# Local attention's values: one product over a mixed block of keys, and two products in halves of TensorE's rows

## The chip, the cores and the metric

The kernel runs on one core of one Trainium2 chip, as one program. The metric is device time in microseconds (us), measured around one execution. Times in the tables come from the runs and from one profiled execution of the kernel before.

## What is computed

A decoder layer over `x` of 4 batches x 512 rows x 512, in three parts, each added to `x`: local attention with 16 heads of 128 that share one key and one value head, cross attention over 1024 context rows, and a ternary feed-forward network. The change touches the first part alone, cut here to what matters:

```python
k = _rmsnorm(_apply_partial_rope(h @ wk, cos, sin), k_norm_w)   # one key head for all 16 heads
v = h @ wv
diff = i[:, None] - i[None, :]
mask = (diff >= 0) & (diff < WIN)                                # WIN = 128
scores = jnp.einsum('bhtd,bsd->bhts', q, k) * scale
scores = jnp.where(mask[None, None], scores, -1e30)
probs = jax.nn.softmax(jnp.concatenate([scores, sink], axis=-1), axis=-1)
attn = jnp.einsum('bhts,bsd->bhtd', probs[..., :t], v)
```

Every row sees the 128 keys that end with itself. In tiles of 128 rows, row t of a tile sees keys 0 to t of its own tile and keys t+1 to 127 of the tile before it: for each place p among 128 exactly one of the two tiles' keys. So one 128x128 block holds all weights of a head's row tile, and the first row tile of a batch has no tile before it.

## The kernel before

The 2048 rows are 16 row tiles of 128, four to a batch. Local attention works in 64 `Unit`s: row tile `t` = n // 4 and head group `g` = n % 4, four heads (`HG`) each; `qt` is the tile's number in its batch. A unit goes through these steps:

- `queries`: `q_ps` (L770), rope on ScalarE and VectorE (L554 to L561), and the reciprocal root of the norm `rs` on GpSimd (L81).
- `turn`: four transposes of q (`qtr`, L780) and a copy `qT` on ScalarE (L782).
- `scores`: `sc` (L789) against the keys of both tiles; `s` takes the own tile's scores (L794) and, where the mask `older` says so, those of the tile before (L795, `neg_sb` in a batch's first tile); then the negative maxima `nm` (L799 to L801).
- `weights`: `p` by exponentials on ScalarE (L811), their sums `den` on VectorE, and the division on GpSimd (L818).
- `turn_weights`: four transposes of p into PSUM (`ptr`, L825); VectorE writes two masked copies, `pT[:, 1]` for keys of the own tile (`newer_t`, L827) and `pT[:, 0]` for keys of the tile before (`older_t`, L829, where `qt > 0`).
- `values`: `av` as the sum of a product with `v[:, qt]` (L834) and, where `qt > 0`, one with `v[:, qt - 1]` (L836); ScalarE copies it into `attnT` (L843).

When four units have filled a tile's `attnT`, `project` makes its output: 16 products `y` (L663), added to `xres` (L667). TensorE's and ScalarE's orders are written out by hand in one loop over n: unit n's `turn`, unit n-1's `weights`, unit n+1's `queries`, unit n's `scores`, unit n-2's `values`, unit n-1's `turn_weights`. `fill` puts pieces of work that is due at any time between them: first the folding of the output weights (L652), later the products `y`. Around `values` the loop reads:

```python
                if n >= 2:
                    units[n - 2].values()
                fill(1 if many else 1 + n % 2)
```

`before(b)` prepares the next batch's `qcT`, keys and `v` in the same loop (L587, `kv_ps` L601, `ktr` L619), `ternary_weights` reads and rounds the feed-forward weights on VectorE (L687 to L717), `mask_rows` has one small product of four rows (L757), and `first_rows` begins cross attention in the last steps (L189, L223, L290). VectorE's and GpSimd's orders are left to the scheduler.

PSUM has eight banks: pool `aq` holds one bank for `q_ps` and `qtr` (tag "q") and one for `ptr` and `av` (tag "p"); `asc` two for `sc`; `af` two for tag "f", which serves the preparation, and two for tag "y". Cross attention, from about 700 us, uses parts of TensorE's array: `weights` there runs four products on 32 rows each (L1051), and `weigh` and `divide` four products with 32 columns each (L1076, L1090).

Of the kernel before, what the change touches and what calls it, by code (L numbers as in the profile page):

```python
# [12 lines left out]
F32 = mybir.dt.float32  # L13
F32R = mybir.dt.float32r
BF16 = mybir.dt.bfloat16
U32 = mybir.dt.uint32
U8 = mybir.dt.uint8
AF = mybir.ActivationFunctionType
ALU = mybir.AluOpType
# [3 lines left out]
P = 128  # L23
# [5 lines left out]
HG = 4  # L29
# [21 lines left out]
def decoder_layer(  # L51
# [7 lines left out]
    nc = tc.nc  # L59
# [66 lines left out]
    def transpose_rows(pool, src, dst, tag="tr", copy=None):  # L126

        ps = pool.tile([P, DC, P], F32, tag=tag, name="tr_ps")
        for c in range(DC):
            nc.tensor.transpose(ps[:, c, :], src[:, ts(c, P)], ident)  # L130
        (copy or nc.scalar.copy)(dst, ps)
# [60 lines left out]
    class KeysValues:  # L192
# [62 lines left out]
        def values(self, quarter):  # L255
            if quarter == 0:
                self.va = values_pool["bp"].tile([P, KT, P], F32, name="va", bufs=2)
            v_ps = some_bank([P, 2, P], "v_ps")
            for i in range(2):
                for c in range(DC):  # L260
                    nc.tensor.matmul(
                        v_ps[:, i, :], lhsT=self.cxT[quarter][:, c, ts(i, P)], rhs=wv_sb[:, c, :],
                        start=(c == 0), stop=(c == DC - 1),
                    )
            nc.scalar.copy(self.va[:, 2 * quarter:2 * quarter + 2, :], v_ps)
# [220 lines left out]
    with tc.tile_pool(name="aw", bufs=1) as aw, tc.tile_pool(name="akv", bufs=2) as akv, \  # L486
# [15 lines left out]
        sin_sb = aw.tile([P, QT, 64], F32, name="sin_sb")  # L502
        nc.sync.dma_start(out=sin_sb, in_=c_sin.rearrange("(t p) n -> p t n", p=P))

        kq_col = aw.tile([P, 2], F32, name="kq_col")
        nc.sync.dma_start(out=kq_col[:, 0:1], in_=k_norm_w.rearrange("(p o) -> p o", o=1))
        nc.sync.dma_start(out=kq_col[:, 1:2], in_=q_norm_w.rearrange("(p o) -> p o", o=1))
        kw_col = aw.tile([P, 1], F32, name="kw_col")
# [9 lines left out]

        older = aw.tile([P, P], F32, name="older")
        nc.gpsimd.memset(older, 0.0)
        nc.gpsimd.affine_select(
            out=older, in_=older, compare_op=ALU.is_ge, fill=1.0, base=0,
            pattern=[[-1, P]], channel_multiplier=1,
        )
        older_t = aw.tile([P, P], F32, name="older_t")
        nc.gpsimd.memset(older_t, 1.0)
        nc.gpsimd.affine_select(
            out=older_t, in_=older_t, compare_op=ALU.is_gt, fill=0.0, base=0,  # L530
            pattern=[[-1, P]], channel_multiplier=1,
        )
        newer_t = aw.tile([P, P], F32, name="newer_t")
        nc.gpsimd.memset(newer_t, 0.0)
        nc.gpsimd.affine_select(
            out=newer_t, in_=newer_t, compare_op=ALU.is_gt, fill=1.0, base=0,
            pattern=[[-1, P]], channel_multiplier=1,
        )
        neg_sb = aw.tile([P, P], F32, name="neg_sb")
        nc.gpsimd.memset(neg_sb, NEG)  # L540

        def heads(ap):
            return ap.unsqueeze(1).to_broadcast([P, HG, P])
# [86 lines left out]
        def fold():  # L630
            w2s = {}

            def turned(n):
                g, h = divmod(n, HG)
                if h == 0:
                    w2s[g] = ap.tile([P, DC, D], F32, name="w2")
                    nc.sync.dma_start(
                        out=w2s[g], in_=out_w2[g * D:(g + 1) * D].rearrange("(c p) o -> p c o", p=P)
                    )
                w1 = ap.tile([P, D], F32, name="w1")  # L640
                nc.sync.dma_start(out=w1, in_=out_w1[g, ts(h, P)])
                w1T = ap.tile([P, DC, P], F32, name="w1T")
                transpose_rows(fp, w1, w1T, tag="y", copy=nc.vector.tensor_copy)
                return w1T

            w1T = turned(0)
            yield
            for n in range(HEADS):
                after = turned(n + 1) if n + 1 < HEADS else None
                f_ps = fp.tile([P, D], F32, tag="y", name="f_ps")  # L650
                for c in range(DC):
                    nc.tensor.matmul(  # L652
                        f_ps, lhsT=w1T[:, c, :], rhs=w2s[n // HG][:, c, :],
                        start=(c == 0), stop=(c == DC - 1),
                    )
                    yield
                nc.scalar.copy(wf[:, n, :], f_ps)
                w1T = after

        def project(t, attnT):  # L660
            y = fp.tile([P, D], F32, tag="y", name="y")
            for h in range(HEADS):
                nc.tensor.matmul(  # L663
                    y, lhsT=attnT[:, h, :], rhs=wf[:, h, :], start=(h == 0), stop=(h == HEADS - 1)
                )
                yield
            nc.vector.tensor_tensor(xres[:, t, :], y, xres[:, t, :], ALU.add)  # L667
# [95 lines left out]
        class Unit:  # L763
# [20 lines left out]
            def scores(self):  # L784
                g, qt, kT = self.g, self.qt, made[self.b][1]
                sc = scp.tile([P, HG, 2 * P], F32, name="sc")
                first = 1 if qt == 0 else 0
                for h in range(HG):
                    nc.tensor.matmul(  # L789
                        sc[:, h, first * P:], lhsT=self.qT[:, h, :],  # L790
                        rhs=kT[:, (qt - 1 + first) * P:(qt + 1) * P], start=True, stop=True,
                    )
                s = a2.tile([P, HG, P], F32, name="s")
                nc.scalar.copy(s, sc[:, :, P:2 * P])  # L794
                nc.vector.copy_predicated(  # L795
                    s, heads(older.bitcast(U32)), heads(neg_sb) if qt == 0 else sc[:, :, 0:P]
                )
                nm = small.tile([P, HG], F32, tag="nm", name="nm")
                nc.vector.tensor_reduce(nm, s, AX.X, ALU.max, negate=True)  # L799
                nc.vector.tensor_tensor(nm, nm, self.rs, ALU.mult)  # L800
                nc.vector.tensor_tensor(nm, nm, nsink_sb[:, ts(g, HG)], ALU.min)  # L801
                es = small.tile([P, HG], F32, tag="es", name="es")
                nc.vector.tensor_tensor(es, nm, sink_sb[:, ts(g, HG)], ALU.add)
                self.s, self.nm, self.es = s, nm, es
# [17 lines left out]
            def turn_weights(self):  # L822
                ptr = qp.tile([P, HG, P], F32, tag="p", name="ptr")
                for h in range(HG):
                    nc.tensor.transpose(ptr[:, h, :], self.p[:, h, :], ident)  # L825
                self.pT = a2.tile([P, 2, HG, P], F32, name="pT", bufs=1)
                nc.vector.tensor_tensor(self.pT[:, 1], ptr, heads(newer_t), ALU.mult)  # L827
                if self.qt > 0:
                    nc.vector.tensor_tensor(self.pT[:, 0], ptr, heads(older_t), ALU.mult)  # L829

            def values(self):
                v, qt = made[self.b][2], self.qt
                av = qp.tile([P, HG, P], F32, tag="p", name="av")
                nc.tensor.matmul(av, lhsT=v[:, qt, :], rhs=self.pT[:, 1], start=True, stop=(qt == 0))  # L834
                if qt > 0:
                    nc.tensor.matmul(  # L836
                        av, lhsT=v[:, qt - 1, :], rhs=self.pT[:, 0], start=False, stop=True
                    )
                if self.g == 0:
                    while self.t - 3 in behind:  # L840
                        fill(1)
                    attnTs[self.t] = a2.tile([P, HEADS, P], F32, name="attnT", bufs=3)
                nc.scalar.copy(attnTs[self.t][:, ts(self.g, HG), :], av)  # L843
                if self.g == G - 1:
                    behind[self.t] = project(self.t, attnTs.pop(self.t))

        attnTs, behind = {}, {"fold": fold()}

        def fill(n):

            for _ in range(n):
                while behind:
                    first = next(iter(behind))
                    if next(behind[first], "end") != "end":
                        break
                    del behind[first]

        with tc.manual_schedule(engines={mybir.EngineType.PE, mybir.EngineType.Activation}):
# [24 lines left out]
            for b in range(1, B):  # L883
                nc.sync.dma_start(
                    out=xres[:, b * QT:(b + 1) * QT, :], in_=x[b].rearrange("(t p) d -> p t d", p=P)
# [73 lines left out]
    with tc.tile_pool(name="b1", bufs=1) as b1, \  # L959
# [208 lines left out]
        for b in range(1, B):  # L1168
            at = KT * HG * (b - 1)
# [114 lines left out]
    with tc.tile_pool(name="c1", bufs=1) as c1, \  # L1284
# [14 lines left out]
        def tile_at(t):  # L1299
            return tiles[t] if 0 <= t < NT else Nothing()  # L1300
# [7 lines left out]
        for s in range(NT + 5):  # L1308
            now, prev, old, older, oldest = (tile_at(s - d) for d in range(5))
# [90 lines left out]
```

## Time and profile before

| | |
|---|---|
| median of 3 runs | 1709.8 us (1709.46 to 1713.5) |
| profiled execution | 1710.19 us, of which the span from first to last instruction is 1708.3 us |
| granted TensorE clock | 0.989 of full speed over the span |
| TensorE busy | 1632.2 us (96%) |
| VectorE, ScalarE, GpSimd busy | 1173.7, 919.8 and 707.8 us |
| `av` products (L834, L836) | 128 and 96 records of 592 ns, first at 73.0, last at 668.2 us |
| copies of `av` (L843) | 64, median 585 ns |
| masked copies (L827, L829) | 64 of 692 ns and 48 of 681 ns (medians) |

PE is TensorE's products, PEld its weight loads, DVE VectorE, ACT ScalarE, POOL GpSimd, SP the engine that issues most transfers. L12 is line 12 of the kernel. A product of f32 operands appears as two records on PE, each with a load on PEld. Ends of matmul records are modelled, so successive records overlap in the profile; the distance between starts tells how long one holds the array. In a timeline row the columns are start, length, engine, line, operation, operands, form and how many records were merged.

### The profile page before, as it was taken

To read this page: it belongs to the slowest core of one execution; us is meant where nothing else is said; L and a number is where in the kernel's file an instruction comes from. 1 tells how busy PE (TensorE), PEld (TensorE's weight loads), DVE (VectorE), ACT (ScalarE), POOL (GpSimd) and SP (SyncE) were. 2 spreads that over 40 slices of the span, in tenths; PEclk is the share of its full clock that TensorE was granted. 3 is DMA by queue.
4 is the path that set the end of the run, shared out by engine and by line. 5 is a ranking of instruction groups with operands and counts; after the bars stand their busy time and mean duration, and the time that the engine had idled before them with its cause. 6 is when DMAs were issued, how large, how long until landed. Compare 5 with 4: busy or idle time off the path is not lost.

```text
span 1708.3 us, 22965 instructions
## 1 busy us (share of the span) xinstructions
PE 1632.2 (96%) x7872; PEld 938.4 (55%) x7904; DVE 1173.7 (69%) x2323; ACT 919.8 (54%) x1807; POOL 707.8 (41%) x458
## 2 busy tenths in 40 slices
PE   7899999999999999899999999999999998999997
PEld 4555555655655555555555555555544435666664
DVE  4556886888787863565656666666657657989997
ACT  1444454555455553134544454445565764888885
POOL 2212222222222221347878787878778930000000
PEclk9999999999999999889999999999999999999999
DMA  8422221322233200412112111221121110000000
GB/s 258 136 88 85 74 75 52 84 81 72 78 74 93 68 1 25 100 54 52 52 32 60 50 47 37 56 54 33 39 69 55 35 57 2 13 13 14 19 19 25
DMA packets 96549, 99.56 MB, mean 58 GB/s; under 512 B 50884, under 2 KB 57672, under 8 KB 96008
## 3 DMA queue, kind: packets, MB, share of 16 engines
q1 hardware_dynamic: 88608, 84.30, 17.3%
q10 hardware_dynamic: 6672, 12.65, 2.3%
q0 software_dynamic: 1152, 1.15, 0.3%
q8 instruction: 62, 1.02, 0.2%
q14 instruction: 55, 0.45, 0.1%
HBM read 61.76 MB, written 10.86 MB: 43 GB/s over the span
## 4 chain that ended last, share of the span: by engine, by line
PE 80%; DVE 7%; ACT 6%; issue 3%; SPq 1%; DMA 1%; POOL 1%; ACTq 0%; POOLq 0%; DVEq 0%
PE y L663 12%; PE s_ps L992 8%; PE st L1040 7%; PE o_ps L1076 6%; PE sc L789 5%; PE q_ps L290 3%; PE f_ps L652 3%; PE xo_ps L1135 3%; PE av L834 3%; PE st L1051 3%; PE q_ps L770 3%; PE av L836 2%; PE y_ps L422 2%; PE d_ps L470 2%; ACT p L1058 2%
## 5 line engine op out<-in xcount | busy, mean ns | idle before, releaser
L1065 POOL TENSOR_TENSOR sum<-sum,p 128x1024 f32<-128x1024 f32 x180 | 423.1, 2377 | 37.3 <-ACT p L1058 37.1
L996 DVE TENSOR_REDUCE nm<-s_ps 128x1 f32<-128x512 f32 x512 | 319.7, 682 | 165.9 <-PE s_ps L992 165.8
L1058 ACT ACTIVATE p<-st 128x1024 f32<-128x1024 f32 x256 | 249.1, 1020 | 86.0 <-PE st L1051 81.8
L663 PE MATMUL y<-wf,attnT 128*128 128x512 f32 x512 | 246.8, 592 | 0.0
L818 POOL TENSOR_TENSOR p<-p,den 128x512 f32<-128x512 f32 x64 | 67.2, 1050 | 407.6 <-DVE den L817 230.1
L992 PE MATMUL s_ps<-ks,qs 99*128 99x512 f32 x512 | 200.1, 460 | 23.3 <-DVE nm L996 13.3
L992 PEld LDWEIGHTS s_ps<-ks,qs 99*128 99x128 f32 x512 | 88.6, 192 | 175.9 <-DVE nm L996 59.9
L1040 PE MATMUL st<-qs,ks 101*128 101x512 f32 x512 | 165.6, 404 | 5.3 <-ACT p L1058 3.8
L1076 PE MATMUL o_ps<-p,va 128*32 128x512 f32 x1024 | 137.3, 605 | 0.7 <-ACT p L1058 0.7
L663 PEld LDWEIGHTS y<-wf,attnT 128*128 128x128 f32 x512 | 91.9, 190 | 73.7 <-issue 71.7
L811 ACT ACTIVATE p<-s,nm,rs 128x128 f32<-128x128 f32 x256 | 123.2, 484 | 8.4 <-DVE nm L801 8.4
L1065 POOL TENSOR_TENSOR sum<-p,p 128x1024 f32<-128x1024 f32 x30 | 70.6, 2374 | 110.8 <-ACT p L1058 97.2
L1040 PEld LDWEIGHTS st<-qs,ks 101*128 101x128 f32 x512 | 95.6, 191 | 36.8 <-ACT p L1058 21.5
L789 PE MATMUL sc<-kT,qT 128*128 128x256 f32 (+1 forms) x512 | 107.6, 353 | 0.0
L789 PEld LDWEIGHTS sc<-kT,qT 128*128 128x128 f32 x512 | 88.8, 190 | 27.2 <-issue 17.9
L81 POOL TENSOR_TENSOR rs<-ss,neghalf 128x4 f32<-128x4 f32 (+1 forms) x72 | 80.2, 1115 | 53.5 <-DVE ss L564 50.8
L782 ACT COPY qT<-qtr 128x512 f32<-128x512 f32 x64 | 37.5, 585 | 114.1 <-PE qtr L780 111.6
L843 ACT COPY attnT<-av 128x512 f32<-128x512 f32 x64 | 37.5, 585 | 101.7 <-PE av L836 84.4
L386 PEld LDWEIGHTS <-xqT 128*128 128x128 bf16 x512 | 50.4, 99 | 48.8 <-issue 3.1
L827 DVE TENSOR_TENSOR pT<-ptr,newer_t 128x512 f32<-128x512 f32 x64 | 44.0, 688 | 43.7 <-PE ptr L825 43.5
L294 ACT ACTIVATE qH<-q_ps 128x256 fp32r<-128x256 f32 x32 | 12.3, 384 | 106.0 <-PE q_ps L290 102.6
L422 PE MATMUL y_ps<-had,mT 128*128 128x128 f32 x512 | 68.7, 282 | 0.0
(195 smaller groups left out, 3030.5 us busy)
## 6 DMA issues: line engine op xcount, KB each, us to landing
cx<-in_ctx SPq DMA_DIRECT2D x32, 256.0 KB
qs<-qH SPq DMA_DIRECT2D x128, 64.0 KB
w<-in_L_attn_out_w SPq DMA_DIRECT2D x4, 1024.0 KB
w<-in_L_attn_out_w SPq DMA_DIRECT2D x16, 256.0 KB
raw<-in_L_ffn_w_gate SPq DMA_DIRECT2D x4, 1024.0 KB
raw<-in_L_ffn_w_up SPq DMA_DIRECT2D x4, 1024.0 KB
raw<-in_L_ffn_w_down SPq DMA_DIRECT2D x4, 1024.0 KB
raw<-in_L_ffn_w_gate ACTq DMA_DIRECT2D x8, 512.0 KB
```

What stands on the lines that cost most here:

```text
L81: nc.gpsimd.tensor_tensor(dst, src, neghalf[:, :src.shape[1]], ALU.pow)
L422: nc.tensor.matmul(y_ps[:, k, :], lhsT=self.mT[q][:, k, :], rhs=had, start=True, stop=True)
L663: nc.tensor.matmul(y, lhsT=attnT[:, h, :], rhs=wf[:, h, :], start=(h == 0), stop=(h == HEADS - 1))
L789: nc.tensor.matmul(sc[:, h, first * P:], lhsT=self.qT[:, h, :], rhs=kT[:, (qt - 1 + first) * P:(qt + 1) * P], start=True, stop=True,)
L811: nc.scalar.activation(self.p[:, h, :], s[:, h, :], AF.Exp, bias=nm[:, h:h + 1], scale=self.rs[:, h:h + 1], accum_out=den[:, h:h + 1],)
L818: nc.gpsimd.tensor_tensor(self.p, self.p, den.unsqueeze(2).to_broadcast([P, HG, P]), ALU.mult)
L992: nc.tensor.matmul(s_ps, lhsT=qss[hh][0:R_TOP, g, ts(qt, P)], rhs=kss[b % 2][0:R_TOP, g, ts(hf, T)], start=True, stop=True,)
L996: nc.vector.tensor_reduce(nms[m][:, qt, g, hf:hf + 1], s_ps, AX.X, ALU.max, negate=True)
L1040: nc.tensor.matmul(st[:, g % 2, :], lhsT=ks[0:R_TOP + 2, g, ts(kt, P)], rhs=qss[hh][0:R_TOP + 2, g, :], start=True, stop=False,)
L1058: nc.scalar.activation(p, st, AF.Exp)
L1065: by.tensor_tensor(sums[m][i], last[i] if kt == 1 else sums[m][i], ps[i], ALU.add)
L1076: nc.tensor.matmul(accs[m][at, :], lhsT=va[:, kt, at], rhs=ps[g // 2][:, g % 2, :], start=(kt == 0), stop=(kt == KT - 1),)
```

## The change

The transposed weights are used in another grouping. Split the 128 key places and the 128 rows of a tile in halves of 64. For rows 0 to 63, places 64 to 127 are all keys of the tile before; for rows 64 to 127, places 0 to 63 are all keys of the own tile. A new tile `mixed`, made once for each row tile with `qt > 0` by two copies on GpSimd, holds the own tile's values in places 0 to 63 and the previous tile's in 64 to 127. One masked copy (`either_t`) leaves in `pT[:, 1]` all weights that go with `mixed`; what remains are two 64x64 corners a head, written to `pT[:, 0]` by two subtractions.

`values` now makes two tiles `av` of 64 rows each for the four heads (256 columns), one in the bank of tag "p", the other in one of tag "f". Two products over all 128 places run against `mixed` (or `v[:, 0]` in a batch's first tile), and where `qt > 0` two more over 64 places each, on partitions 0 to 63 and 64 to 127. ScalarE copies the two tiles with two instructions. The mask `older_t` goes, and the constant `neg_sb` becomes one column of `kq_col`, read with a broadcast.

```diff
-        older_t = aw.tile([P, P], F32, name="older_t")
...
+        either_t = aw.tile([P, P], F32, name="either_t")
+        nc.vector.tensor_copy(either_t[0:64], newer_t[0:64])
+        nc.vector.tensor_scalar(either_t[64:P], newer_t[64:P], -1.0, 1.0, ALU.mult, ALU.add)
+        neg_sb = kq_col[:, 2:3]
...
-                nc.vector.tensor_tensor(self.pT[:, 1], ptr, heads(newer_t), ALU.mult)
+                nc.vector.tensor_tensor(
+                    self.pT[:, 1], ptr, heads(either_t if self.qt > 0 else newer_t), ALU.mult
+                )
                 if self.qt > 0:
-                    nc.vector.tensor_tensor(self.pT[:, 0], ptr, heads(older_t), ALU.mult)
+                    for at in (slice(0, 64), slice(64, P)):
+                        nc.vector.tensor_tensor(
+                            self.pT[at, 0, :, at], ptr[at, :, at], self.pT[at, 1, :, at],
+                            ALU.subtract,
+                        )
...
-                av = qp.tile([P, HG, P], F32, tag="p", name="av")
-                nc.tensor.matmul(av, lhsT=v[:, qt, :], rhs=self.pT[:, 1], start=True, stop=(qt == 0))
+                if self.g == 0 and qt > 0:
+                    mixed[0] = a2.tile([P, P], F32, name="mixed", bufs=1)
+                    nc.gpsimd.tensor_copy(mixed[0][0:64], v[0:64, qt])
+                    nc.gpsimd.tensor_copy(mixed[0][64:P], v[64:P, qt - 1])
+                avs = [
+                    pool.tile([P, HG, 64], F32, tag=tag, name="av")
+                    for pool, tag in ((qp, "p"), (fp, "f"))
+                ]
+                halves = slice(0, 64), slice(64, P)
+                for av, at in zip(avs, halves):
+                    nc.tensor.matmul(
+                        av, lhsT=mixed[0] if qt > 0 else v[:, 0, :], rhs=self.pT[:, 1, :, at],
+                        start=True, stop=(qt == 0),
+                    )
                 if qt > 0:
-                    nc.tensor.matmul(
-                        av, lhsT=v[:, qt - 1, :], rhs=self.pT[:, 0], start=False, stop=True
-                    )
+                    for av, at, of in zip(avs, halves, (qt - 1, qt)):
+                        nc.tensor.matmul(
+                            av, lhsT=v[at, of, :], rhs=self.pT[at, 0, :, at], start=False, stop=True
+                        )
...
-                nc.scalar.copy(attnTs[self.t][:, ts(self.g, HG), :], av)
+                for av, at in zip(avs, halves):
+                    nc.scalar.copy(attnTs[self.t][:, ts(self.g, HG), at], av)
```

In the changed kernel the products over all places are on line 849, those over 64 places on line 855, the copies on line 863, the subtractions on line 832 and the copies for `mixed` on lines 841 and 842.

More of the change, by code (lines that the diff above doesn't have):

```diff
@@ L503, in decoder_layer @@
         nc.sync.dma_start(out=sin_sb, in_=c_sin.rearrange("(t p) n -> p t n", p=P))
-        kq_col = aw.tile([P, 2], F32, name="kq_col")
+        kq_col = aw.tile([P, 3], F32, name="kq_col")
         nc.sync.dma_start(out=kq_col[:, 0:1], in_=k_norm_w.rearrange("(p o) -> p o", o=1))
@@ L526, in decoder_layer @@
         )
-        older_t = aw.tile([P, P], F32, name="older_t")
[L528 to L531, printed above, removed]
-        )
         newer_t = aw.tile([P, P], F32, name="newer_t")
@@ L538, in decoder_layer @@
         )
-        neg_sb = aw.tile([P, P], F32, name="neg_sb")
+        either_t = aw.tile([P, P], F32, name="either_t")
+        nc.vector.tensor_copy(either_t[0:64], newer_t[0:64])
+        nc.vector.tensor_scalar(either_t[64:P], newer_t[64:P], -1.0, 1.0, ALU.mult, ALU.add)
+        neg_sb = kq_col[:, 2:3]
         nc.gpsimd.memset(neg_sb, NEG)
@@ L795, in scores @@
                 nc.vector.copy_predicated(
-                    s, heads(older.bitcast(U32)), heads(neg_sb) if qt == 0 else sc[:, :, 0:P]
+                    s, heads(older.bitcast(U32)), neg_sb.unsqueeze(1).to_broadcast([P, HG, P]) if qt == 0 else sc[:, :, 0:P]
                 )
@@ L826, in turn_weights @@
                 self.pT = a2.tile([P, 2, HG, P], F32, name="pT", bufs=1)
-                nc.vector.tensor_tensor(self.pT[:, 1], ptr, heads(newer_t), ALU.mult)
+                nc.vector.tensor_tensor(
+                    self.pT[:, 1], ptr, heads(either_t if self.qt > 0 else newer_t), ALU.mult
+                )
                 if self.qt > 0:
-                    nc.vector.tensor_tensor(self.pT[:, 0], ptr, heads(older_t), ALU.mult)
+                    for at in (slice(0, 64), slice(64, P)):
[3 more added lines that the diff above has]
+                        )
             def values(self):
                 v, qt = made[self.b][2], self.qt
-                av = qp.tile([P, HG, P], F32, tag="p", name="av")
-                nc.tensor.matmul(av, lhsT=v[:, qt, :], rhs=self.pT[:, 1], start=True, stop=(qt == 0))
+                if self.g == 0 and qt > 0:
[12 more added lines that the diff above has]
+                    )
                 if qt > 0:
-                    nc.tensor.matmul(
-                        av, lhsT=v[:, qt - 1, :], rhs=self.pT[:, 0], start=False, stop=True
-                    )
+                    for av, at, of in zip(avs, halves, (qt - 1, qt)):
+                        nc.tensor.matmul(
+                            av, lhsT=v[at, of, :], rhs=self.pT[at, 0, :, at], start=False, stop=True
+                        )
                 if self.g == 0:
@@ L842, in values @@
                     attnTs[self.t] = a2.tile([P, HEADS, P], F32, name="attnT", bufs=3)
-                nc.scalar.copy(attnTs[self.t][:, ts(self.g, HG), :], av)
+                for av, at in zip(avs, halves):
+                    nc.scalar.copy(attnTs[self.t][:, ts(self.g, HG), at], av)
                 if self.g == G - 1:
                     behind[self.t] = project(self.t, attnTs.pop(self.t))
-        attnTs, behind = {}, {"fold": fold()}
+        attnTs, behind, mixed = {}, {"fold": fold()}, {}
         def fill(n):
```

## The prediction

> **What bounds the kernel now.** I read the page's engine totals first, then the busy time by stretches of the stage that the change touches, then TensorE's waits there, and then single instructions in order of time.
>
> ```profile
> PE 1632.2 (96%) x7872; PEld 938.4 (55%) x7904; DVE 1173.7 (69%) x2323; ACT 919.8 (54%) x1807; POOL 707.8 (41%) x458
> ```
> ```profile
> core 0: us, PE busy (x) PEld busy (x) DVE busy (x) ACT busy (x) POOL busy (x), PEclk, DMA share, GB/s
> 130.00:290.00 160.00, 159.00 (x579) 92.54 (x578) 117.78 (x304) 79.69 (x242) 39.49 (x38) 1.00 0.21 73
> 290.00:440.00 150.00, 148.73 (x546) 86.87 (x545) 120.47 (x305) 78.83 (x244) 39.96 (x37) 1.00 0.27 76
> 440.00:590.00 150.00, 149.30 (x538) 86.09 (x537) 121.38 (x317) 79.32 (x245) 41.23 (x40) 1.00 0.30 81
> ```
> ```profile
> engine line waited for: us in total, times, longest us
> PE qc_ps L587 <- ACT hT L131: 2.0, 2, 1.0
> PE qtr L780 <- DVE q L561: 1.0, 3, 0.4
> ```
> The change lies in local attention, up to 670 us. There TensorE is busy over 99% of each stretch at full clock, VectorE about 80%, ScalarE 53%, GpSimd 27%. Between 130 and 650 us TensorE waits 3.0 us for other engines. So time here is TensorE's instruction stream: what it gains or loses passes into the total, and work on the others is hidden until TensorE waits for it.
>
> Two passages of TensorE's timeline give the prices: one from this stage, one from cross attention, where products use row and column groups of the array.
>
> ```profile
> 360.28 1.02 PE L834 MATMUL av<-pT,v 128*128 128x512 f32 x2
> 361.14 1.02 PE L836 MATMUL av<-pT,v 128*128 128x512 f32 x2
> 362.00 1.02 PE L663 MATMUL y<-wf,attnT 128*128 128x512 f32 x2
> 362.93 0.63 PE L825 MATMUL ptr<-ident,p 128*128 128x128 f32 x4
> 363.48 0.38 PE L757 MATMUL some_ps<-ident,some 4*128 4x4 f32 x2
> 363.79 0.66 PE L780 MATMUL qtr<-ident,q 128*128 128x128 f32 x4
> ...
> 366.86 1.89 PE L789 MATMUL sc<-kT,qT 128*128 128x256 f32 x8
> ```
> ```profile
> 1005.81 0.59 PE L290 MATMUL q_ps<-h2T,wq_sb 128*128 128x256 f32 x2
> 1006.34 0.50 PE L1051 MATMUL st<-qL,kL 32*128 32x512 f32 x4
> 1006.77 1.06 PE L1076 MATMUL o_ps<-p,va 128*32 128x512 f32 x8
> 1007.77 0.96 PE L992 MATMUL s_ps<-ks,qs 99*128 99x512 f32 x3
> 1008.57 0.62 PE L1040 MATMUL st<-qs,ks 101*128 101x512 f32 x2
> ```
> Starts count, since ends are modelled. An f32 product of 512 columns is two records 0.86 us together (360.28 to 361.14), so 0.43 a record; one of 256 columns is two of 0.216 (eight in 1.89 us, the last lasting 0.379: 1.51/7).
>
> **What a unit's products cost now.** In 48 of the 64 units (three of four row tiles) two 512-column products run: 360.28 to 362.00, 1.72 us.
>
> **What they cost afterwards.** Full rows: two products of 256 columns, 4 x 0.216 = 0.864. Then the array goes to two halves of 64 rows and back; no row shows 64 rows, so I price it by the nearest rows. Into row groups: the last L290 record starts at 1005.81 + 0.59 - 0.38 = 1006.02 and fills until 1006.24, yet L1051 starts at 1006.34: 0.10 lost. L1051's four records (one pass) start together, and the next form starts 0.43 later; one such pass takes 0.23 (L1040's pair: 0.62 less a record of 0.395). The 0.20 over is the next change's 0.10 and 0.10 of weight load that nothing hides. Back to the full array: L1076's two passes take 2 x 0.43 = 0.86, but L992 starts 1.00 later, and its three records last 0.96 where 0.395 + 2 x 0.235 = 0.865 is usual: 0.10 for the change, 0.10 for the load. So each change costs 0.20, the pair 0.40. L757 in this very stage, one f32 product on four rows and four columns, holds the array 0.31 us, with another 0.1 ahead of it: the same price.
>
> The halves themselves are two products of 256 columns, two records each. L1076 is four f32 products in four column groups: eight records in 1.06 us where one product's pair takes 0.43 + 0.592 = 1.02. First records run together, then second ones. If row halves do the same, they take 2 x 0.216 = 0.43; run one after the other, 0.86. They write different banks, as L1051's do, so I take 0.43.
>
> Sum: 0.864 + 0.40 + 0.43 = 1.69 against 1.72, about -0.02 a unit, **-1.0 us** in 48 units. What overlap saves (0.43), the changes cost (0.40). The other 16 units split one product by columns, 4 x 0.216 against 2 x 0.43: nothing.
>
> The Trainium skill has a rule against this change: "TensorEngine Tiling (Array Packing)", section Key Properties, says that changing the tiling mode drains TensorE. The trace agrees (the 0.10 above). Another page, "TensorE: Matmul & The Clock Gate", section Part 3: Packing small matmuls, lets packed matmuls span one duration plus about 4 ns for each further tile; by that alone the sum would be some 20 us lower, and L1051's 0.43 for a pass of 0.23 differs.
>
> **Waits around it.** ptr and av share one bank, so the transposes at L825 wait for the attnT copy.
>
> ```profile
> 308.45 1.02 PE L663 MATMUL y<-wf,attnT 128*128 128x512 f32 x2
> ...
> 308.65 0.58 ACT L843 COPY attnT<-av 128x512 f32<-128x512 f32 x1 [1.99 <-PE av L836]
> ...
> 309.35 0.42 PEld L825 LDWEIGHTS ptr<-ident,p 128*128 128x128 f32 x4 [0.71 <-issue]
> 309.38 0.63 PE L825 MATMUL ptr<-ident,p 128*128 128x128 f32 x4
> ```
> One output product (308.45 + 0.86 = 309.31) just fails to cover copy and signal: 0.07 us idle, in the half of the units with one product there. Afterwards the transposes wait only for the first of two copies of 256 columns (0.37 us, as L607's v copy) instead of 0.58, and the product starts 0.2 later: the gap goes, 24 x 0.07 = **-1.5 us** (between -1.8 and 0).
>
> ScalarE: 64 x (2 x 0.37 - 0.585) = +10 us, in an engine 47% idle, first copy earlier: 0; without that cover 0.16 a unit. VectorE: one 0.68 us product with a mask becomes two subtractions of 256 columns on 64 partitions, nearest L558 at 0.405: +0.1 a unit. TensorE waits for VectorE only three times; **+0.5 us**, between 0 and 48 x 0.1 = 5.
>
> GpSimd: 12 x 2 copies of 64x128 for "mixed". Nearest rows are L753 (12x2048 in 1.88 us) and L612 (128x256, two inputs, 0.61), so 0.12 to 0.6 each; I take 0.25. In the built program's order they stand behind the weights (L818) of their own unit or earlier, in the step before the one that uses them, some 9 us ahead. They first wait until the preceding unit's products have read the old "mixed". Queued behind them is the next rs (L81), needed by the maxima one step later: 0.
>
> The second half of av takes turns in pool "f" with the buffers of the preparation. In the built order TensorE then waits for kv_ps' rope only at the next preparation product, 10 us on; in the last three units context transposes and keys wait for an av copy, mostly behind 1.7 us of output products: **+0.5 us** (0 to 3). At the start the second normalisation stands behind either_t on VectorE, which waits for newer_t on GpSimd, now after the four rstd (9.4 us): tile 1 comes up to 1 us later, but tile 3, which ends that chain, no longer waits for the kq_col load at 11.11: 0 (-0.4 to +1). The removed mask and shorter constant: 0.
>
> Total: -1.0 - 1.5 + 0.5 + 0.5 = **-1.5 us**. The profiled execution took 1710.2 us (span 1708.3, 1.9 around it): 1708.7. The median of the runs, 1709.8, is 0.4 lower: **1708.4 us**, within 0.3% (5.1 us), which is about what a measurement of this kernel tells from no change.
>
> **Rivals.**
> 1. *The halves don't overlap in full (slower).* If records issue strictly in order, half one's second record waits for its first, half two's first joins it, and half two's second runs alone: three slots instead of two, 48 x 0.216 = +10.4: 1718.8. With no overlap, so that the change doesn't do what it says, +20.7: 1729. For it: no row shows two-record products in row groups (L1051 has one each). Against it: L1076's eight records. It decides early: with 0.43 saved and 0.40 paid, losing a third of the overlap (0.14 a unit, 6.6 us) takes the sum from -1.5 over the 0.3%. Chances 0.17 and 0.10. The skill's page on TensorE (same section) says that matmuls start and end strictly in program order; by that rule, and two adjacent records a product, it is the three slots. L1076 speaks against that reading.
> 2. *The changes of form are cheaper with half rows (faster).* At no cost, -0.40 x 48 = -19: 1689; at half, 1699. For: 64 rows were never seen. Against: all three kinds of change seen cost the same. Chance 0.15.
> 3. *TensorE waits for "mixed".* If the copies fell behind the next unit's weights, whose L818 ends up to 2.4 us after av starts (327.43 against 325.07), then with 0.6 us for copies and signal eight of the twelve tiles would be late, by 0.3 to 3.0 us, 10.5 in all: 1718.9. The built order speaks against it. Chance 0.06.
>
> **How the numbers follow.** The forecast has 0.52, with 1704 (each change 0.05 cheaper, 96 x 0.05 = 4.8) to 1713 (VectorE at its upper bound, 4.5 more) as its own range. 8 in 10 need the three slots, rival 3 and the nearer part of rival 2 as well: 1701 to 1721. Faster by over 0.3%: rival 2 and the forecast's lower tail (0.04), 0.19. Slower: rivals 1 and 3 and the upper tail (0.04), 0.37. Within: 0.44.
>
> **What would show it.** In the profile afterwards: L855's records of both halves starting within nanoseconds in two pairs about 0.32 apart (0.216 and the 0.10 of load); 0.10 idle before them and 0.10 after; from the first av record to the next y 1.69 us; y to ptr without gap; TensorE not waiting for GpSimd. L855 starting in three or four steps, or under 0.6 us from its first start to the next y's (I have 0.73), would prove me wrong.

## The result, and the profile after

The changed kernel takes 1706.8 us (median of 13 runs) where the kernel before takes 1711.3 us (13 runs): ratio 0.9975, 95% interval 0.9966 to 0.9984. That is 4.4 us less, inside the 0.3% that the forecast called no change, and more than the 1.5 us of its sum. The profiled execution has a span of 1704.7 us against 1708.3, with the same granted clock, 0.989.

The totals, then busy time in the three stretches of local attention (same columns as before):

```profile
PE 1630.1 (96%) x8096; PEld 956.6 (56%) x8128; DVE 1184.3 (69%) x2373; ACT 926.3 (54%) x1871; POOL 715.1 (42%) x480
```
```profile
130.00:290.00 160.00, 158.84 (x636) 97.36 (x635) 122.11 (x317) 81.80 (x263) 41.76 (x44) 1.00 0.22 73
290.00:440.00 150.00, 148.56 (x607) 92.64 (x606) 123.34 (x323) 79.87 (x259) 43.55 (x44) 1.00 0.27 76
440.00:590.00 150.00, 149.52 (x607) 91.53 (x606) 122.84 (x330) 80.68 (x261) 42.75 (x46) 1.00 0.30 81
```
TensorE is as full as before (over 99%), at full clock; VectorE has 1.5 to 4.3 us more in each stretch, ScalarE up to 2.1, GpSimd up to 3.6, and none of them has become the bound. TensorE's waits between 130 and 650 us:

```profile
PE qc_ps L587 <- ACT hT L131: 2.0, 2, 1.0
PE qtr L780 <- DVE q L561: 0.6, 3, 0.3
PE ptr L825 <- POOL p L818: 0.3, 1, 0.3
PE ptr L825 <- ACT attnT L863: 0.2, 1, 0.2
PE tr_ps L189 <- ACT h L117: 0.2, 1, 0.2
```
No wait for `mixed`, and less waiting for VectorE's q (0.6 for 1.0). One unit in order of time:

```profile
305.69 1.03 PE L849 MATMUL av<-pT,mixed 128*128 128x256 f32 x4
...
306.65 0.70 PE L855 MATMUL av<-pT,v 64*128 64x256 f32 x4
...
307.28 1.12 PE L663 MATMUL y<-wf,attnT 128*128 128x512 f32 x2
307.38 0.37 ACT L863 COPY attnT<-av 128x256 f32<-128x256 f32 x1 [1.76 <-PE av L855]
...
308.25 0.60 PE L825 MATMUL ptr<-ident,p 128*128 128x128 f32 x4
```
Four full-row records of 0.216 end at 306.55; L855 starts at 306.65, 0.09 later (0.309 from the last L849 record's start in each of the 48 units). Its four records are two pairs: in this trace's records the two halves start 6 to 7 ns apart, the second pair 0.32 after the first, where 0.216 is streaming and 0.104 the load. y follows 0.306 later (0.216 and 0.09), and its first record lasts 0.697 where the others last 0.592, another 0.104 of load. So 1.59 us from the first av record to y, and 0.104 inside y: 1.69 us, against 1.72. The transposes follow y without a gap (307.28 + 0.53 + 0.43 = 308.25).

### The profile page after: what moved, and what is told of

Same layout as the page of the kernel before. It is cut to its first block, busy times and chain, and to the rows that moved or that the text cites. A ratio compares the mean times of both kernels' runs of the same rounds, so it can differ in the third digit from the quotient of the medians.

```text
span 1704.7 us, 23538 instructions
## 1 busy us (share of the span) xinstructions
PE 1630.1 (96%) x8096; PEld 956.6 (56%) x8128; DVE 1184.3 (69%) x2373; ACT 926.3 (54%) x1871; POOL 715.1 (42%) x480
## 4 chain that ended last, share of the span: by engine, by line
PE 79%; DVE 9%; ACT 7%; issue 3%; POOL 1%; DMA 1%; SPq 0%; ACTq 0%; POOLq 0%; DVEq 0%
PE y L663 11%; PE s_ps L1012 8%; PE st L1060 7%; PE o_ps L1096 6%; PE sc L789 5%; PE q_ps L290 3%; PE f_ps L652 3%; PE xo_ps L1155 3%; PE st L1071 3%; PE av L849 3%; PE q_ps L770 3%; PE y_ps L422 2%; PE d_ps L470 2%; PE u_ps L386 2%; PE g_ps L386 2%
## 5 line engine op out<-in xcount | busy, mean ns | idle before, releaser
L663 PE MATMUL y<-wf,attnT 128*128 128x512 f32 x512 | 251.7, 602 | 0.0
L663 PEld LDWEIGHTS y<-wf,attnT 128*128 128x128 f32 x512 | 88.0, 190 | 61.6 <-issue 59.1
L863 ACT COPY attnT<-av 128x256 f32<-128x256 f32 x128 | 42.8, 377 | 86.6 <-PE av L855 74.7
L652 PE MATMUL f_ps<-w,w1T 128*128 128x512 f32 x128 | 63.2, 605 | 5.6 <-ACT wf L657 3.6
```

The lines of the kernel that those rows point to most:

```text
L652: nc.tensor.matmul(f_ps, lhsT=w1T[:, c, :], rhs=w2s[n // HG][:, c, :], start=(c == 0), stop=(c == DC - 1),)
L663: nc.tensor.matmul(y, lhsT=attnT[:, h, :], rhs=wf[:, h, :], start=(h == 0), stop=(h == HEADS - 1))
```

## The experiments

Two theories stood at first. Mine: the overlap of the halves (0.43 us a unit) is paid back by the two changes of form, from full rows to halves and back (0.39), and what shows is this small remainder and the waits around it. The rivals: half rows or changes of form cost something else than the gaps beside them say; or the time comes from elsewhere (the split copies alone, the start).

**The split copies alone.** Before's masks and products; only the two tiles av and their copies are new.

```diff
+                for av, at in zip(avs, halves):
+                    nc.tensor.matmul(
+                        av, lhsT=v[:, qt, :], rhs=self.pT[:, 1, :, at], start=True, stop=(qt == 0)
+                    )
+                if qt > 0:
+                    for av, at in zip(avs, halves):
+                        nc.tensor.matmul(
+                            av, lhsT=v[:, qt - 1, :], rhs=self.pT[:, 0, :, at], start=False, stop=True
+                        )
```


> The kernel before, with one part of the change alone: av is split into two tiles of 64 queries a head (one in pool p, one in pool f), each with its own copy; the products still take all 128 rows of keys with the old masks, now as four products of 256 columns (8 records x 0.216 = 1.73 us, as before's 1.72). Theory (products give -1.1, waits around them the rest): y to ptr loses its 0.07 us gaps (about -1.6), the late waits for the f bank come (+0.6), so some -1 to -3 us against before, and 1 us more than the changed kernel. Rival (the whole gain comes from the overlapped halves): no change against before. Rival (the gain lies in what VectorE no longer does, or in the start): no change in local attention, since masks and start are the old ones.

Measured: 1708.4 us, ratio 0.9982 (0.9973 to 0.9991), 3.1 us less than before. By the medians, then, the halves don't bring all of the gain. The trace doesn't put the 3.1 us into local attention: from 69 to 673 us, by the same instructions in both traces, this kernel loses 0.2 us against before, where the changed kernel gains 2.5. The idle time between output products and ptr sinks from 1.7 to 0.7 us, but TensorE waits longer for VectorE's q than before (2.3 us for 1.0), 1.1 us of it at once, between 530 and 560 us:

```profile
PE qtr L780 <- DVE q L561: 2.3, 5, 1.1
```
Its span is 1.9 us shorter than before's for what happens in the last 20 us: before TensorE's last product this execution has 3.4 us at half clock there and before's 6.8. So it isn't shown that the split copies alone save time in local attention.

**Corners over full rows.** The corners get a buffer whose other blocks stay zero; no half rows, no change of form.

```diff
-                            av, lhsT=v[at, of, :], rhs=self.pT[at, 0, :, at], start=False, stop=True
+                            av, lhsT=v[:, of, :], rhs=corner[:, :, at], start=False, stop=True
```


> The changed kernel, but the two corner products take all 128 rows: the corners lie in a buffer of their own whose other blocks stay zero, so no half rows and no change of form. Everything else of the change (mixed, the split copies, the subtractions) stays. Theory: the overlap saves 0.43 us a unit and the changes of form cost 0.41, so that without both the unit takes 8 x 0.216 = 1.73 in place of 1.69: about +1.1 to +1.6 us against the changed kernel, ratio to before near 0.998. Rival (changes of form are far cheaper than the 0.2 that I read from starts, since ends are modelled): up to +20 us, 1727. Rival (the form changes delay TensorE in places that the starts beside them don't show): faster than the changed kernel.

Measured: 1706.8 us, ratio 0.9971 (0.9960 to 0.9983): the same as the changed kernel to 0.02 us. TensorE's timeline:

```profile
366.63 1.03 PE L851 MATMUL av<-pT,mixed 128*128 128x256 f32 x4
367.49 1.03 PE L857 MATMUL av<-corner,v 128*128 128x256 f32 x4
368.36 1.88 PE L665 MATMUL y<-wf,attnT 128*128 128x512 f32 x4
```
1.73 us a unit, no gaps, y's records at their usual length: 0.034 us more than the changed kernel's 1.69. The 1.6 us that makes in 48 units lies within the runs' scatter. So half rows with their changes of form are worth nothing that whole runs can tell here; the rival of 20 us falls. In the trace the stage (69 to 673 us) gains 0.7 us against before where the changed kernel gains 2.5, so 1.8 for the half rows, close to the 1.6 of the starts. The whole span doesn't show it, because this execution was 1.9 us further ahead at 69 us and, like that of the split copies, had 3.4 us at half clock near its end where the changed kernel's had 6.8.

**Both corners on the same rows.** The second corner's product reads the first's rows; the second corner's own weights are left out.

```diff
-                    for av, at, of in zip(avs, halves, (qt - 1, qt)):
+                    at = halves[0]
+                    for av, of in zip(avs, (qt - 1, qt)):
```


> The changed kernel, with both corner products on rows 0 to 63 (the second one multiplies the first corner's weights in place of its own, so the second half's output is wrong by that part). As many half-row products, the same changes of form, the same banks. Theory: products on the same rows can't run together, so the halves take 4 x 0.216 where they took 2 x 0.216: +0.43 us a unit, +20.7 us in 48, about 1727.5, ratio to before 1.0097. Rival (records of two products run together because they write different banks, whatever rows they use): no change, 0.9975. Rival (three slots, of which the changed kernel already paid one): +10.4.

Measured: 1724.7 us, ratio 1.0081 (1.0068 to 1.0095): 17.8 us over the changed kernel.

```profile
366.12 1.03 PE L849 MATMUL av<-pT,mixed 128*128 128x256 f32 x4
367.08 1.13 PE L856 MATMUL av<-pT,v 64*128 64x256 f32 x4
368.14 1.12 PE L663 MATMUL y<-wf,attnT 128*128 128x512 f32 x2
```
From first av record to y 2.014 us in place of 1.589: +0.425, as expected, 20.4 us in 48 units; the gaps before and after L856 are the old ones. Records now start one by one (0.32, then 0.216 apart). So the two products overlap only on different rows here, and the changed kernel has all of the overlap. Of the 20.4 us the stage shows 19.1 (against before, +16.6 between 69 and 673 us where the changed kernel has -2.5): longer units leave less to wait for.

**The corners apart.**

```diff
-                for av, at in zip(avs, halves):
+                for av, at, of in zip(avs, halves, (qt - 1, qt)):
...
-                    for av, at, of in zip(avs, halves, (qt - 1, qt)):
+                    if qt > 0:
```


> The changed kernel with the four products in another order: full first half, its corner, full second half, its corner. The same products, two pairs of changes of form a unit in place of one, and the corners no longer together. Theory: +0.43 for the lost overlap and +0.41 for the second pair of changes, 0.84 us a unit, +40 us in 48: 1747, ratio to before 1.021. Rival (a change of form costs little, and the idle 0.1 us at L855 and the next y are something that comes once a unit, such as the switch to another bank or the loads): +20.7 us, ratio 1.0097. Rival (corners need not be neighbours to be cheap): no change.

Measured: 1742.7 us, ratio 1.0186 (1.0172 to 1.0200): 35.9 us over the changed kernel.

```profile
365.09 0.59 PE L849 MATMUL av<-pT,mixed 128*128 128x256 f32 x2
365.62 0.70 PE L854 MATMUL av<-pT,v 64*128 64x256 f32 x2
366.24 0.70 PE L849 MATMUL av<-pT,mixed 128*128 128x256 f32 x2
366.87 0.70 PE L854 MATMUL av<-pT,v 64*128 64x256 f32 x2
367.50 1.13 PE L663 MATMUL y<-wf,attnT 128*128 128x512 f32 x2
```
From the second pair on, each pair of records takes 0.62 to 0.63 us where it streams for 0.43: every change of form costs 0.19 to 0.20, in both directions, and the second L849 pays it as L854 does. 2.41 us in place of 1.59, 39 us in 48 units; the stage shows 37.7. The rival that puts the idle time down to something that comes once a unit falls.

**Two units at a time.** If a pair of changes costs 0.39 whatever lies between, two units should share one. The values of groups g and g+1 run in one step; products of 512 columns; one set of changes.

```diff
+                if self.g % 2 == 0:
+                    pair[0] = a2.tile([P, 2, HG, P], F32, name="pT", bufs=1)
+                    pair[1] = a2.tile([P, 2, HG, 64], F32, name="corner", bufs=1)
...
-                    pool.tile([P, HG, 64], F32, tag=tag, name="av")
+                    pool.tile([P, 2, HG, 64], F32, tag=tag, name="av")
...
-                if n >= 2:
+                if n >= 3 and n % 2:
                     units[n - 2].values()
```


> The changed kernel, with the values of two units (groups g and g+1 of one row tile) in one step, every other step: the full-row products have 512 columns (two units), then the four corner products of both units become two of 512 columns, then two copies of 128x512. The same columns stream, but there is one pair of changes of form for two units. Theory: two units take 8 x 0.429/2 = 1.72 full rows, 0.39 for the changes, 2 x 0.429 = 0.86 for corners, 2.97 us in place of 3.39: 24 x 0.42 = 10 us less than the changed kernel, about 1697, ratio to before 0.9915. Rival (form changes are cheap; what I read beside them is a fixed fill of each product): no change. Rival (steps without values last 7.4 us, and VectorE, with some 7.3 us of work a step, is late for them): the gain is eaten by TensorE's waits for q and for pT.

Measured: 1702.1 us, ratio 0.9949 (0.9936 to 0.9961): 4.8 us under the changed kernel, 8.9 under before; the fastest of all, and half of what was expected.

```profile
364.60 1.88 PE L852 MATMUL av<-pT,mixed 128*128 128x512 f32 x4
366.41 1.13 PE L858 MATMUL av<-corner,v 64*128 64x512 f32 x4
367.47 1.98 PE L663 MATMUL y<-wf,attnT 128*128 128x512 f32 x4
```
```profile
PE ptr L825 <- POOL p L818: 1.9, 4, 0.7
PE qtr L780 <- DVE q L561: 1.0, 3, 0.4
```
2.87 us and 0.104 in y, 2.97 for two units: the price holds, 10 us in all. But the idle time between output products and ptr rises from 0.8 to 3.4 us, mostly the waits for GpSimd's p, and that between ptr and qtr from 1.1 to 2.3. A step without values now takes some 6.9 us in place of 8.6, which may be too short for GpSimd and VectorE. That is argued: the edit (cut above) also gives p one buffer in place of two, in all runs with pairs, and no run separates the two.

Its control takes the half rows away and keeps the pairs:

```diff
-                            av, lhsT=v[at, of, :], rhs=pair[1][at], start=False, stop=True
+                            av, lhsT=v[:, of, :], rhs=pair[1][:, :, :, at], start=False, stop=True
```


> The kernel with the values of two units in one step, but corners over all 128 rows, from a buffer whose other blocks stay zero: no half rows, no change of form. It tells the pairing's own effect from what half rows bring. Theory: two units take 16 x 0.216 = 3.44 us, as before the change; so 24 x 0.47 = 11 us more than the pairs with half rows, and within 2 us of the full-row kernel without pairs (ratio to before 0.997 to 0.999). Rival (pairing by itself brings or costs time, by waits): this kernel moves with the pairs by the same amount, and the difference of the two is then still the half rows' worth.

Measured: 1713.2 us, ratio 1.0009 (1.0000 to 1.0019): 11.2 us over the pairs with half rows, as expected, and 6.4 over full rows without pairs. Half rows earn 11 us with one pair of changes for two units, where by the starts they earn 1.6 with one for each. The starts say the same: two units take 3.434 us in place of 2.974, and 24 x 0.46 = 11.0, so that the one buffer for s, which this edit (cut above) has in place of two, needs no part in it. Pairing itself, with its single buffer for p, costs time: 6 us by the medians, 3.2 in the stage of the traces (2.5 over before, where full rows without pairs are 0.7 under).

**More work on VectorE.** Each subtraction is done twice.

```diff
+                        nc.vector.tensor_tensor(
+                            self.pT[at, 0, :, at], ptr[at, :, at], self.pT[at, 1, :, at],
+                            ALU.subtract,
+                        )
```


> The changed kernel with each corner subtraction done twice (same result): VectorE gets 0.84 us more a unit, 48 x 0.84 = 40 us over local attention, which takes its busy share there from 82% to about 89%. Theory (the change's +0.16 us a unit on VectorE is hidden, since TensorE waits for VectorE five times only): 0 to +5 us against the changed kernel, most of it in the last units, where av waits for the subtraction. Rival (VectorE is close to being the bound, and part of its extra work shows): +20 us or more.

Measured: 1718.2 us, ratio 1.0040 (1.0026 to 1.0053): 11.3 us over the changed kernel.

```profile
PE av L853 <- DVE pT L836: 6.0, 7, 1.6
```
Of 40 us a good quarter shows, more than my theory had and less than the rival's 20; VectorE's share between 130 and 590 us is 85% (391.8 us of 460) for 80%. av takes over the bank of ptr, which the subtraction reads, and waits for it. VectorE's reserve covers the change's own 8 us (48 x 0.16) and most of 40 us more, but not all.

**Shifting output products between the steps of the pairs.** Three versions; each moves fills of one output product.

```diff
-                fill(2 if many else 1)
+                fill(2 if many else 1 - n % 2)
...
-                fill(1 if many else 1 + n % 2)
+                fill(1 if many else 2)
```


> The pairs with half rows, with one output product moved from each step that holds the values to each step without: 5 and 4 products in place of 4 and 5, so that the steps' lengths on TensorE differ by 1.2 us less than 3. Theory: the same TensorE work, so the same time as the pairs (ratio 0.9915) if they show no waits, and less if TensorE waits in the shorter steps. Rival (order doesn't matter since the stage is bound by TensorE's stream alone): no difference from the pairs.

Measured: 1710.5 us, ratio 0.9996 (0.9987 to 1.0005), 8.5 us over the pairs. The second version has the first line of this edit, and `1 + 2 * (n % 2)` in the last:

> The pairs with half rows again, with one output product moved within the steps that hold the values: from between scores and values to behind the values, so that three output products in place of two stand between the values and the transposes of the weights (ptr), which take over av's bank. The number of products in each step stays 4 and 5. In the pairs TensorE lost 3.4 us between output products and ptr (2.6 more than in the changed kernel), waiting for the attnT copy, now of 512 columns, and for GpSimd's p. Theory: the copy's waits go, GpSimd has 0.86 us more in every other step: -1.5 to -3 us against the pairs, 1699 to 1700.5, ratio to before near 0.9935. Rival (the loss moves to the next product that needs the engines that are behind): no change against the pairs.

Measured: 1712.9 us, ratio 1.0006 (0.9997 to 1.0015). In both a wait appears that neither before nor the pairs had (this line is the second version's):

```profile
PE q_ps L770 <- ACT qT L782: 6.6, 9, 0.7
```
A tile's 16 products were used up one step early, and nothing was left to put between qtr and q_ps. I had not counted them over four steps. The third version gives each step without values one product less:

```diff
-                fill(2 if many else 1)
+                fill(2 if many else 0)
...
-                fill(1 if many else 1 + n % 2)
+                fill(1 if many else 1 + 2 * (n % 2))
```


> The pairs with half rows and three output products behind the values, as in the run before, but with 3 products in each step without values in place of 4, so that a tile's 16 products last until the next tile's begin (3 + 3 + 5 + 3 + 2). In the run before they were used up one step early, and TensorE then stood between qtr and q_ps for 0.9 us nine times. Theory: those 8 us are back, and the waits between output products and ptr go as they did there (0.2 in place of 3.4 us): -1.5 to -3 us against the pairs, some 1699 to 1701, ratio to before near 0.994. Rival (a step without values now lasts some 6 us, and GpSimd's p or VectorE's q come late there): the pairs' time or more, 1702 to 1708, with TensorE waiting for p or q in these steps.

Measured: 1707.5 us, ratio 0.9975 (0.9966 to 0.9985), 5.5 over the pairs. The waits between qtr and q_ps are gone, and the rival holds: TensorE now waits, from 130 to 650 us, 3.3 us for VectorE's q (1.0 in the pairs), 2.5 for GpSimd's p (1.9) and 1.9 for VectorE's corners (none). The pairs as they were run first stay the best version.

**The start.** The removed mask is built again, or the new start is put into the kernel before.

```diff
+        nc.gpsimd.memset(either_t, 1.0)
+        nc.gpsimd.affine_select(
+            out=either_t, in_=either_t, compare_op=ALU.is_gt, fill=0.0, base=0,
+            pattern=[[-1, P]], channel_multiplier=1,
+        )
```


> The changed kernel with the start's GpSimd work as before: the mask that the change removed (a memset and a select of 128x128) is built again ahead of newer_t, and then overwritten by either_t. Theory (the change's start differs only by when loads land: the second normalisation waits for x, 6.6 to 7.5 us, in kernels with either start): no change, 1706.8, within 1 us. Rival (the removed mask is what brings the 1 to 2 us that the sum doesn't have): +1 to +2 us.

Measured: 1704.9 us, ratio 0.9963 (0.9951 to 0.9976), 1.9 us less than the changed kernel, with overlapping intervals; its stage gains 2.3 us against before, as the changed kernel's 2.5. The removed mask brings nothing.

```diff
+        older_t = aw.tile([P, P], F32, name="older_t")
+        for at in (slice(0, 64), slice(64, P)):
+            nc.vector.tensor_scalar(older_t[at], newer_t[at], -1.0, 1.0, ALU.mult, ALU.add)
+        neg_sb = kq_col[:, 2:3]
```


> The kernel before with the start of the changed one: older_t is made on VectorE from newer_t in two operations of 64 rows, as either_t is, and the constant for the first tiles is one column. Local attention is as before. Theory: no change against before, within 1 us. Rival (the start is what brings the 1 to 2 us that the sum doesn't have): -1 to -2 us, ratio 0.999.

Measured: 1710.9 us, ratio 0.9999 (0.9990 to 1.0008): nothing either. Its trace shows what becomes of a lead: this kernel runs 1.08 us ahead of before from 55 to 392 us, instruction by instruction, and 0.02 behind from 400 us on. Near 395 us TensorE waits 0.7 us for VectorE's q (before 0.3) and 0.4 for GpSimd's p. The split copies lose 1.0 in the same place; the changed kernel, with 0.5 us of waits there, keeps most of its lead (1.9 us at 387, 1.6 at 399).

## Why the prediction was right, point by point

- **Products (-1.0).** -0.024 us a unit in all 48, -1.1 us. Each piece measured what the rows of before had said: 0.216 a record, the halves together in 0.43, 0.09 idle before and after, 0.104 of load twice. L855 to y took 0.63 us, not my 0.73: the load after the change lies inside y's first record. One reading was off: for the way back, L1076's row gives 1.00 less 0.86, so 0.14, where I wrote 0.10; here it is 0.09. Rival 1 (no or part overlap) falls by the pairs of records and by the same-rows run; rival 2 (cheaper changes with 64 rows) by the corners apart and the pairs. The Trainium skill's rule on draining, in "TensorEngine Tiling (Array Packing)", section Key Properties, agrees with the 0.09. The Trainium skill's span rule in "TensorE: Matmul & The Clock Gate", section Part 3: Packing small matmuls, has about 4 ns for a further tile; what lies between the changes comes near it (7 ns for the second half), but the rule leaves out the 0.39 around it, which is nearly all of the 0.43 that the overlap saved.
- **y to ptr (-1.5).** The gaps of 0.07 are gone, -1.7 us. Two new waits (by starts 0.44 for GpSimd's p and 0.34 with attnT's copy) give 0.8 back.
- **VectorE (+0.5).** The two subtractions take 0.42 us each for one product of 0.68, +0.16 us a unit, not +0.1 (by starts 0.89 for 0.60, where the next instruction follows at once). It stays hidden up to 650 us; the doubled subtractions show that the cover has an end.
- **Late waits (+0.5).** They came to +0.7 (the lead over before falls from 3.7 us at 662 to 3.0 at 672), but by another mechanism, so that the size was right by luck. In the last unit av waits for VectorE:

```profile
663.92 1.10 PE L849 MATMUL av<-pT,mixed 128*128 128x256 f32 x4 [0.81 <-DVE pT L832]
```
```profile
662.33 0.68 DVE L667 TENSOR_TENSOR xres<-y,xres 128x512 f32<-128x512 f32 x1
662.92 0.85 DVE L832 TENSOR_TENSOR pT<-ptr,pT 64x256 f32<-64x256 f32 x2
```
VectorE does y's addition ahead of the subtractions, which read ptr's bank, and av needs that bank. The corners over full rows wait the same 0.8 us, and there the subtractions write a tile that the waiting product doesn't read. I had looked at the second half's bank "f" alone.
- **ScalarE, GpSimd, `mixed` (0).** No wait of TensorE for any of them that before didn't have, but for the two above and 0.2 us for h (L117). Rival 3 falls.
- **Start (0, -0.4 to +1).** -0.4 us at 69 us in the profiled execution. That is within what executions differ by: in the ten other profiled kernels with the new start TensorE stood between -2.3 and +0.8 us there.

Where the sum was short: local attention as a whole, by the same instructions in both traces, brings -2.5 us (offset -0.4 at 69 us, -3.0 at 673). The products, y to ptr (net -0.9), shorter waits for q (-0.4), less time inside ptr's transposes (-0.6) and the late wait make -2.3; 0.2 I couldn't put down to single gaps. The rest of the 4.4 lies outside: -0.4 in the start; -0.8 later, where before has a wait of 1.1 us for a load ahead of L1040 that the changed kernel's trace doesn't have; and 0.7 because before's profiled execution was 1.1 us under its median and the changed kernel's 0.4. None of these is tied to the change by a run, and a kernel that differs from the changed one by two hidden instructions came out 1.9 us lower. So -2.5 is shown for the change, and whether it does more stays open.

That 1708.4 came as near to 1706.8 as it did is in part luck: the sum was 2.9 us short, and the three runs that I started from had a median 1.5 us under that of the 13.

## What to carry to other kernels

Half rows save what they overlap and pay about 0.39 us for each excursion out of full rows and back: the time of some 230 columns of an f32 product here (0.86 us for 512). Two halves that overlap save as much once each has 230 columns; a unit has 256. Count the columns that lie between two changes before splitting, and put as many half-row products as banks and buffers allow into one excursion; with one unit it was nearly a wash, with two it was worth 11 us. And when TensorE's work is moved between steps, count the filler and the other engines' work of each step by itself: an engine at 80% of the stage may become the bound in a step that got a fifth shorter.

## What the hardware showed that I had not expected

An f32 product is two records, and with two row halves the order is first records together, then second records together, 6 to 7 ns apart, although the kernel writes one product after the other. The load after a change of form shows as a longer first record (0.480 for 0.376 us in the halves, 0.697 for 0.592 in y), in each of the 96 changes.

Executions of the same kernel scatter with the granted clock: the changed kernel's 13 spans go from 1701.9 us at 0.991 to 1708.5 at 0.986, about 1.1 us for each 0.001 by a line through all 13; the 6.6 us between the ends are more than the effect of most edits above. In the traces the clock isn't a little lower throughout: it is full except for stretches at half. Near the end, before's execution has it at 0.50 from 1695.2 to 1702.0 us; the execution of the split copies has it at 0.50 from 1690.4 to 1693.8 only, and gains 1.9 us on before between 1685 and 1702. So a difference of a few us between two executions is read stage by stage.
